# A graph network on 64 graphs: one channel into the stored inputs, loads and a product later, the end of the gates half a graph later

## The chip, the cores and the metric

The kernel runs on one core of a Trainium2 chip. The metric is the device time of one execution in microseconds, as the median of several runs. Beside it there is a profile of one execution. Its engines are TensorE (PE; its weight loads are listed as PEld), VectorE (DVE), ScalarE (ACT), GpSimd (POOL) and SyncE (SP), which only issues DMAs. ACT, POOL and SP each have a queue of DMAs of their own. An engine works through its instructions in the order in which they were put, and a wait stops all that is behind it on this engine.

## The reference

There are 64 graphs of 256 nodes with 256 features each, in float32, and a weighted adjacency matrix for each graph. Layer 0 is a graph convolution with a residual and a norm. Layer 1 has a convolution branch, a distance-weighted message, and a GRU cell. Cut to what matters:

```python
# layer 0
deg = adj.sum(-1);  d = where(deg != 0, deg, 1) ** -0.5
h  = (d[:, :, None] * adj * d[:, None, :] + alpha * eye) @ x
x1 = layernorm(x + h @ W.T + b)
# layer 1, on x1
c  = relu(bn1(conv1(x1)))            # conv1: one tap
c  = relu(bn2(conv2(c)) + x1)        # conv2: 17 taps along the nodes
se = x1 @ w_se.T + b_se              # 3 coordinates per node
A  = exp(-sqdist(se, se)) * adj
m  = A @ relu(x1 @ w_msg.T + b_msg)
h2 = GRU(input=[c, m], state=x1)     # w_ih: 768 x 512, w_hh: 768 x 256
out = layernorm(x1 + h2)
```

## The kernel before

**Stages.** The graphs are worked through one by one (`graphs`), in four quarters of 16 (`Q`). For each graph the first part of the work is layer 0 and then, of layer 1, conv1, the coordinates, the distances and the messages. conv2 is done in the frequency domain, for the 16 graphs of a quarter at once: each graph leaves its transformed columns in `VM`, and when a quarter is complete a long stretch multiplies them with the spectrum of the taps (the products `p_k`, L589, with a block `u` of the spectrum streamed from DRAM by `load_u`, L581, six buffers deep), and transforms back into `xc_d` in DRAM (L782). The spectrum `ud` is made at the start, in the first 280 us, between the first graphs (`taps` loaded by SyncE, products on TensorE, stores by GpSimd). Last come the gates of each graph (`gru`): a product of 256 x 768 by 768 x 1024 (hidden and input weights together), done as seven products of halves instead of eight (`p1`, `p7`, `p6`, `p5` and their like, all at L930; the sums of halves of the inputs on GpSimd at L901, the sums of results on VectorE at L948, L958, L964, L1004).

**Inputs of the gates.** A graph's state and message, transposed, lie in a tile `xn` of 128 x 4 x 256, which ScalarE's queue stores to `xn_d` (L568) at the end of the graph. SyncE loads them later into `inputs` (`load_gate`, L840); it also loads the conv branch (`load_conv`, L830 or L836) and the state untransposed (`load_x1`, L848). While `xn` is in use its first channel of the first row holds ones instead of the state's channel 0, which serve as a row of biases in the products. For 36 of the graphs the residual x1 is added to the conv branch by an accumulating DMA (L860), and TensorE transposes it (L885). For the other 28, which `in_blocks` names (the first four of each quarter and the whole last one), VectorE transposes blocks of 32 x 32 (L872, L874), and GpSimd adds the transposed state out of `inputs` (L875). Channel 0 has ones there and not the state; so it is loaded apart into a tile `channel` (L844) and added by GpSimd (L876), and the bias of the ReLU behind it is one less in this channel (`less_one`).

**The end of the gates.** ScalarE makes the tanh of the candidate (L993); VectorE mixes it with the state (L989 to L995), then takes the norm's statistics (L353, L354); GpSimd takes the power (L356), ScalarE applies the norm (L364), and its queue stores the result (L908). The norm's second part is done in the gates of the graph that follows (`ended`).

**What sets the order.** The pieces are generators. `merge` and `paced` interleave the gates of one quarter with the graphs of the next, so that TensorE has matmuls of the one while the other's chains run: the first quarter's transform goes on beside graphs 16 to 21 (280 to 400 us), the second's and third's beside late gates (555 to 780, 1060 to 1270 us), the early gates beside paced graphs (780 to 1060, 1270 to 1570 us), and gates 36 to 47 beside the end of the last transform (1635 to 1806 us). Gates 48 to 63 come alone, at 14.0 us each, from 1806 us to the end. `tc.issue_after` puts an instruction behind a named one in the order of the same engine. In the first 280 us the weights of the gates are loaded as well (`gate_weights`: 16 pieces of `wall` at L1160, L1161 and L1164, then `hh_top`, `gate_bias` twice and `bn_t`, all on SyncE), taken in stages by the list `others` between the graphs; VectorE folds `hh_top` into `wall` (L1180, L1181) and the biases (L1183, L1184).

Of the kernel before, what the change touches and what calls it, by code (L numbers as in the profile page):

```python
# [14 lines left out]
P = 128  # L15
# [5 lines left out]
def bcast_rows(v, n, rows=P):  # L21

    return bass.AP(tensor=v.tensor, offset=v.offset, ap=[[0, rows], [1, n]])
# [3 lines left out]
def kernel(  # L27
# [79 lines left out]

    def load_x(g):
        xin[g] = loads.tile([P, NCH, D], F32, name="x_t")
        nc.sync.dma_start(xin[g], x[g].rearrange("(c p) f -> p c f", p=P))  # L110

    def load(g):
        if g < B:
# [55 lines left out]
    bn_t = const.tile([P, D], F32)  # L169

    bn2_bias = const.tile([P, DCH], F32)
    less_one = const.tile([P, DCH], F32)

    def batch_norms(pool):

# [197 lines left out]
    xn_d = [dram.tile([P, 2 * DCH, N], F32, name=f"xn_d{g}") for g in range(B)]  # L373
    XN = {}
    ALONE = set()
    EXP, WEIGHED, NORMED = {}, {}, []
    gate = None
    EAGER = {0, Q - 4, Q - 3, Q - 2, *range(Q, Q + 13), 2 * Q + 5, 2 * Q + 6, 3 * Q + 5, 3 * Q + 6}
# [95 lines left out]
    def layer1(g, place):  # L474
# [9 lines left out]
        for c in range(NCH):  # L484
            p = bank("p_conv1")[:, : D + NSE]
            for k in range(DCH):
                nc.tensor.matmul(  # L487
                    p, x1T[:, k, c * P : (c + 1) * P], wc1[:, k, :], start=k == 0, stop=k == DCH - 1
                )
            nc.scalar.activation(  # L490
                h[:, c].rearrange("p (k a) -> p k a", k=DCH), p[:, :D].rearrange("p (a k) -> p k a", k=DCH), AF.Relu
            )
            EVICTED[g] = nc.scalar.copy(cols[:, c, :, :NSE], p[:, D:].unsqueeze(1).to_broadcast([P, 4, NSE])).ins
# [71 lines left out]
                    start=mc == 0, stop=mc == NCH - 1,  # L565
                )
        AGGREGATED[g] = nc.scalar.copy(xn[:, 1 : 1 + DCH], p).ins
        nc.scalar.dma_start(xn_d[g], xn)  # L568
        yield


# [4 lines left out]

    TILES, AWAY = [V], []

    def load_u(n, i):
        u = ustream.tile([P, DCH, D], F32, name="u")  # L580
        nc.sync.dma_start(  # L581
            u, ud[i][n * GC : (n + 1) * GC].rearrange("c g o -> (c g) o")[:D].rearrange("(p k) o -> p k o", k=DCH)
        )
        return u

    def product(p, j, v, u, onto=False):
# [225 lines left out]
            yield from output(q, n + 12, im + 3, re + 3)  # L812


    GATE, CONV, SUMS, OWN, CHANNEL = {}, {}, {}, {}, {}


    EARLY = 4

    def in_blocks(g):  # L820
        return g % Q < EARLY or g >= B - Q

    def load_conv(g):
        y = xc_d[g // Q][g % Q]
        if in_blocks(g):


            CONV[g] = gate.tile([P, DCH, N // RB, RB], F32, name="xc_blocks", tag="xc_g")
            for b in range(NB):
                nc.sync.dma_start(  # L830
                    CONV[g][b * RB : (b + 1) * RB],
                    y.rearrange("(s r) (k b j) -> b r k s j", r=RB, k=DCH, j=RB)[b],
                )
            return
        CONV[g] = gate.tile([P, NCH, D], F32, name="xc_g")
        nc.sync.dma_start(CONV[g], y.rearrange("(c p) d -> p c d", p=P))  # L836

    def load_gate(g):
        inputs = GATE[g] = gate.tile([P, 3 * DCH, N], F32, name="inputs")
        nc.sync.dma_start(inputs[:, : 2 * DCH], xn_d[g])  # L840
        if in_blocks(g):
            CHANNEL[g] = gate.tile([1, N], F32, name="channel", bufs=1)
            with nc.allow_non_contiguous_dma("one channel"):
                nc.sync.dma_start(CHANNEL[g], x1_d[g // Q][g % Q][:, 0:1].rearrange("n d -> d n"))  # L844

    def load_x1(g):
        OWN[g] = gate.tile([P, NCH, D], F32, name="x1_g")
        nc.sync.dma_start(OWN[g], x1_d[g // Q][g % Q].rearrange("(c p) d -> p c d", p=P))  # L848

    def sent(g):  # L850

# [12 lines left out]
    def transposed(g):  # L864

        inputs = GATE[g]
        xcT = inputs[:, 2 * DCH :]
        if in_blocks(g):
            to = xcT.rearrange("p k (s r) -> p k s r", r=RB)
            if g < B - Q:  # L870
                with tc.issue_after(WEIGHED[max(WEIGHED)]):
                    nc.vector.transpose(to, CONV.pop(g))  # L872
            else:
                behind(nc.vector.transpose(to, CONV.pop(g)))  # L874
            nc.gpsimd.tensor_tensor(xcT, xcT, inputs[:, 0 : 2 * DCH : 2 * DCH - 1], op=ALU.add)  # L875
            JOINED.append(nc.gpsimd.tensor_tensor(xcT[0:1, 0], xcT[0:1, 0], CHANNEL.pop(g), op=ALU.add).ins)  # L876
            with tc.issue_after(EXP[max(EXP)]):
                for k in range(DCH):
                    nc.scalar.activation(xcT[:, k], xcT[:, k], AF.Relu, bias=less_one[:, k : k + 1])
            return  # L880
        xc = CONV.pop(g)
        p = bank("p_xcT").rearrange("p (k n) -> p k n", k=DCH)
        for k in range(DCH):
            for c in range(NCH):
                nc.tensor.transpose(p[:, k, c * P : (c + 1) * P], xc[:, c, k * P : (k + 1) * P], ident)  # L885
        for k in range(DCH):
            nc.scalar.activation(xcT[:, k], p[:, k], AF.Relu, bias=bn2_bias[:, k : k + 1])
# [17 lines left out]
    def normed(g, part, y, parts=None):  # L905

        yield from layernorm(y, 4 * LN_EPS, None, parts)
        nc.scalar.dma_start(out[g].rearrange("(c p) d -> p c d", p=P)[:, part], y)  # L908

    def ended():  # L910
        while NORMS:
# [2 lines left out]
    def gru(g):  # L914
# [10 lines left out]
        def product(a, b, p=None):  # L925
            first = p is None
            if first:
                p = accbank("p_g")
            for k in range(HALF):
                nc.tensor.matmul(  # L930
                    p[:, : 3 * HD] if k == 0 else p[:, HD:], a[:, k], wall[:, b, k].rearrange("p t d -> p (t d)"),
                    start=first and k == 0, stop=True, skip_group_check=not first or k > 0,
                )
            return p
# [8 lines left out]
        yield  # L943
        if following:
            sent(g + 1)
        p6 = product(S[2], T2)
        mark(nc.vector.tensor_add(quarter(0, 1), first, p6), 1)  # L947
        nc.vector.tensor_add(quarter(1, 1), quarter(0, 1), p7)  # L948
        product(A12, B21, p1)
# [29 lines left out]
        def mixed(part, cols=slice(0, 2)):  # L979
            both = G[:, part, cols].rearrange("p c h t d -> p (c h) t d")  # L980
            chunks = G[:, part].shape[1]
            r, z, n, i = (both[:, :, j, :] for j in (GR, GZ, GN, GI))
            nc.vector.scalar_tensor_tensor(n, r, 1.0, n, op0=ALU.add, op1=ALU.mult)
            i4 = i.rearrange("p (c h) d -> p c h d", c=chunks)
            bias = bn_t.rearrange("p (h d) -> p h d", h=2)[:, cols]
            nc.vector.tensor_tensor(
                i4, i4, bias.unsqueeze(1).to_broadcast([P, chunks, bias.shape[1], HD]), op=ALU.add
            )
            nc.vector.scalar_tensor_tensor(i, n, 0.5, i, op0=ALU.mult, op1=ALU.add)  # L989
            y = x1[:, part]  # L990
            yq = y.rearrange("p c (h d) -> p c h d", h=2)[:, :, cols].rearrange("p c h d -> p (c h) d")
            mark(nc.vector.scalar_tensor_tensor(yq, z, 3.0, yq, op0=ALU.add, op1=ALU.mult), 1)
            nc.scalar.activation(i, i, AF.Tanh)  # L993
            nc.vector.scalar_tensor_tensor(i, z, 1.0, i, op0=ALU.subtract, op1=ALU.mult)  # L994
            nc.vector.tensor_sub(yq, yq, i)  # L995
            return y

        def finished(part, y):
            NORMS.append(normed(g, part, y))
            next(NORMS[-1])  # L1000

        if g < B - 1:
            squashed(1)
# [118 lines left out]
    with tc.tile_pool(name="setup", bufs=1) as setup:  # L1122
# [31 lines left out]
        nc.gpsimd.tensor_copy(wmsg[0:1, 0], biases[:, NSE:])  # L1154

        def gate_weights():
            for b, i, h in ((B11, 0, 0), (T1, 0, 1), (B21, 1, 0), (B22, 1, 1)):
                at = slice(h * HD, (h + 1) * HD)
                own = w_hhT[i * P : (i + 1) * P].rearrange("p (t d) -> p t d", t=3)
                nc.sync.dma_start(wall[:, b, 0, 0:1], own[:, 2:3, at])  # L1160
                nc.sync.dma_start(wall[:, b, 0, 1:3], own[:, 0:2, at])  # L1161
                for k in range(DCH):
                    row = (D if i == 0 else 0) + k * P
                    nc.sync.dma_start(  # L1164
                        wall[:, b, 1 + k], w_ihT[row : row + P].rearrange("p (t d) -> p t d", t=3)[:, :, at]
                    )
            nc.gpsimd.tensor_copy(less_one, bn2_bias)
            nc.gpsimd.tensor_tensor(less_one[:, 0:1], less_one[:, 0:1], unit, op=ALU.subtract)
            top = setup.tile([P, 3, 2, HD], F32, name="hh_top", tag="taps", bufs=2)
            nc.sync.dma_start(top.rearrange("p t h d -> p (t h d)"), bcast_rows(w_hhT, 3 * D))  # L1170
            rows = setup.tile([1, 2, 3, 2, HD], F32, name="gate_bias", tag="taps", bufs=2)
            for i, v in enumerate((b_hh, b_ih)):
                nc.sync.dma_start(rows[:, i].rearrange("p t h d -> p (t h d)"), v.rearrange("(a d) -> a d", a=1))
            nc.sync.dma_start(bn_t, bcast_rows(b_ih[2 * D :], D))
            yield

            for b, i, h in ((B11, 0, 0), (T1, 0, 1), (B21, 1, 0), (B22, 1, 1)):
# [14 lines left out]
        more_weights = gate_weights()  # L1192
        others = [weights(setup, i, scale2) for i in range(NPARTS)]
        others[0] = later(others[0])
        others += [take(more_weights, i) for i in (1, 3, 2)]
        run(graphs(0, range(Q), others))
    ustream = ctx.enter_context(tc.tile_pool(name="ustream", bufs=6))

# [156 lines left out]
```

## Time and profile before

| | |
|---|---|
| median of 3 runs | 2042.55 us (2040.06 to 2043.63) |
| the profiled execution's own time | 2048.04 us |
| its span in the trace | 2046.3 us |
| TensorE busy, matmuls | 1984.9 us, 8157 |
| VectorE, ScalarE, GpSimd busy | 1396.4, 964.7, 698.1 us |
| DMA: bytes, mean rate | 298.05 MB, 146 GB/s |
| granted TensorE clock | 0.994 |

The profiled execution is one run more, with the recorder on; its span goes from its first to its last instruction, and 1.7 us of its time lie around the span. Busy time of TensorE is modelled at the ends of matmuls, so that matmuls which follow each other closely overlap in the listing, and a stall of TensorE is longer by some tenths than the idle time that is listed.

### The profile page before, as it was taken

How to read it: one execution, taken by the hardware profiler on the slowest of the kernel's cores; microseconds unless marked ns; L12 is line 12 of the kernel's file. 1: busy time of each engine (PE TensorE's matmuls, PEld its weight loads, DVE VectorE, ACT ScalarE, POOL GpSimd, SP SyncE). 2: the span in 40 equal slices, each digit the busy share in tenths (PEclk: the TensorE clock that was granted, in tenths of full speed). 3: DMA queues.
4: the chain of work that ended last, by engine and by line, in shares of the span. 5: the costliest groups of instructions: out<-in, count | busy, mean ns of one | idle time of the engine just before them, and what ended most of it. 6: DMA issues, size and time to landing. Idle time of an engine off the chain costs nothing. (4 is left out here: it accounts for less than half of the span.)

```text
span 2046.3 us, 26391 instructions
## 1 busy us (share of the span) xinstructions
PE 1984.9 (97%) x8157; PEld 1437.7 (70%) x8157; DVE 1396.4 (68%) x3199; ACT 964.7 (47%) x2285; POOL 698.1 (34%) x679
## 2 busy tenths in 40 slices
PE   7999999999999999999999999999999999999997
PEld 6878788878667766777777766777777855555554
DVE  6334447787567788764546888874445899877787
ACT  5666654567442234566653233556664233333333
POOL 4444411232532143223322234322331045445543
PEclk8999999999999999999999999999999999999999
DMA  4766557544555654343336665334344745443431
GB/s 133 221 202 207 182 193 240 169 140 135 138 149 192 212 126 134 115 129 109 103 109 185 211 170 134 119 117 125 97 116 142 259 124 135 127 100 87 102 87 54
DMA packets 269021, 298.05 MB, mean 146 GB/s; under 512 B 84276, under 2 KB 211336, under 8 KB 268882
## 3 DMA queue, kind: packets, MB, share of 16 engines
q1 hardware_dynamic: 208842, 200.37, 33.8%
q10 hardware_dynamic: 44472, 67.39, 9.3%
q0 software_dynamic: 15568, 28.62, 6.3%
q8 instruction: 66, 1.08, 0.2%
q14 instruction: 73, 0.60, 0.1%
HBM read 193.19 MB, written 103.06 MB: 145 GB/s over the span
## 5 line engine op out<-in xcount | busy, mean ns | idle before, releaser
L930 PE MATMUL p_g<-wall,sums 128*128 128x384 f32 x1536 | 534.0, 488 | 6.1 <-POOL sums L901 3.2
L930 PEld LDWEIGHTS p_g<-wall,sums 128*128 128x128 f32 x1536 | 284.8, 190 | 193.4 <-issue 9.6
L930 PE MATMUL p_g<-wall,inputs 128*128 128x384 f32 x1152 | 406.8, 489 | 12.2 <-DVE G L948 12.2
L930 PEld LDWEIGHTS p_g<-wall,inputs 128*128 128x128 f32 x1152 | 215.3, 190 | 167.2 <-DVE G L948 27.8
L356 POOL TENSOR_TENSOR ln_rs<-ln_rs,neg_half 128x2 f32<-128x2 f32 x129 | 95.2, 738 | 546.7 <-DVE ln_rs L355 411.0
L901 POOL TENSOR_TENSOR sums<-inputs 128x384 f32<-128x384 f32 x128 | 143.1, 1118 | 329.0 <-PE p_g L930 303.2
L554 DVE TENSOR_TENSOR aT<-aT,adjT 128x512 f32<-128x512 f32 x64 | 45.2, 706 | 200.5 <-ACT aT L551 200.4
L435 POOL TENSOR_TENSOR x_t<-x_t,b_t 128x512 f32<-128x512 f32 x64 | 101.9, 1592 | 215.3 <-ACT x L432 138.8
L589 PE MATMUL p_k<-u,VM 128*128 128x256 f32 x736 | 169.6, 380 | 2.8 <-DMA u<-ud 1.6
L589 PEld LDWEIGHTS p_k<-u,VM 128*128 128x128 f32 x736 | 138.5, 190 | 25.6 <-PE p_k L589 2.5
L364 ACT ACTIVATE x_g<-x_g,ln_mr,ln_rs 128x256 f32<-128x256 f32 x128 | 70.0, 593 | 169.4 <-DVE ln_mr L360 164.6
L977 ACT ACTIVATE G<-G 128x512 f32<-128x512 f32 (+1 forms) x129 | 81.0, 628 | 128.7 <-DVE G L1004 91.9
L440 PE MATMUL p_hT<-adjT,x 128*128 128x256 f32 x512 | 125.7, 389 | 5.8 <-ACT x L432 2.3
L487 PE MATMUL p_conv<-wc,xn 128*128 128x259 f32 x512 | 126.5, 389 | 4.2 <-ACT xn L471 3.5
L563 PE MATMUL p_nmp<-aT,msg 128*128 128x256 f32 x512 | 121.4, 380 | 2.2 <-DVE aT L554 2.2
L450 PE MATMUL p_out<-w,hT 128*128 128x256 f32 x512 | 121.5, 380 | 0.9 <-ACT hT L445 0.7
L901 POOL TENSOR_TENSOR sums<-inputs,sums 128x384 f32<-128x384 f32 x64 | 74.8, 1169 | 138.0 <-PE p_g L930 137.9
L508 PE MATMUL p_msg<-wmsg,xn 128*128 128x256 f32 x512 | 121.9, 381 | 0.0
L487 PEld LDWEIGHTS p_conv<-wc,xn 128*128 128x128 f32 x512 | 99.1, 194 | 27.1 <-ACT xn L471 4.3
L526 PE MATMUL p_dft<-fwd,h 128*128 128x240 f32 x512 | 114.1, 366 | 0.0
L950 ACT COPY G<-p_g 128x512 f32<-128x512 f32 x64 | 37.4, 584 | 155.9 <-PE p_g L930 107.2
L450 PEld LDWEIGHTS p_out<-w,hT 128*128 128x128 f32 x512 | 95.6, 190 | 21.2 <-ACT hT L445 2.9
(173 smaller groups left out, 3596.9 us busy)
## 6 DMA issues: line engine op xcount, KB each, us to landing
u<-ud SPq DMA_DIRECT2D x284, 256.0 KB
xn_d<-xn ACTq DMA_DIRECT2D x64, 512.0 KB
inputs<-xn_d SPq DMA_DIRECT2D x64, 512.0 KB
ud<-u_set POOLq DMA_DIRECT2D x39, 480.0 KB, 6.3
adj_t<-in_adj_dram SPq DMA_DIRECT2D x64, 256.0 KB
x_t<-in_x_dram SPq DMA_DIRECT2D x64, 256.0 KB
x_d<-x ACTq DMA_DIRECT2D x64, 256.0 KB
xc_d<-VM SPq DMA_DIRECT2D x64, 256.0 KB
```

The costliest lines, as they stand in the source:

```text
L356: nc.gpsimd.tensor_tensor(rs[:, : len(chunks)], rs[:, : len(chunks)], neg_half[:, : len(chunks)], op=ALU.pow)
L435: nc.gpsimd.tensor_tensor(x_t, x_t, b0_t.unsqueeze(1).to_broadcast([P, NCH, D]), op=ALU.add)
L440: nc.tensor.matmul(p[:, k, :], x1[:, mc, k * P : (k + 1) * P], adjT[:, mc, 1 - mc : 3 - mc, :].rearrange("p n q -> p (n q)"), start=mc == ...
L450: nc.tensor.matmul(p[:, c, :], hT[:, k, c * P : (c + 1) * P], w0[:, k, :], start=k == 0, stop=k == DCH - 1)
L487: nc.tensor.matmul(p, x1T[:, k, c * P : (c + 1) * P], wc1[:, k, :], start=k == 0, stop=k == DCH - 1)
L508: nc.tensor.matmul(p[:, c, :], x1T[:, k, c * P : (c + 1) * P], wmsg[:, k, :], start=k == 0, stop=k == DCH - 1)
L526: nc.tensor.matmul(p[:, t0 * FL : t1 * FL], h[:, c, k * P : (k + 1) * P], fwd[:, first : first + t1 - t0, :].rearrange("p t f -> p (t f)") ...
L563: nc.tensor.matmul(p[:, k, :], msg[:, mc, k * P : (k + 1) * P], aT[:, mc].rearrange("p n q -> p (n q)"), start=mc == 0, stop=mc == NCH - 1,)
L589: nc.tensor.matmul(p[:, j * D : (j + 1) * D], v[:, k, :], u[:, k, :], start=k == 0 and j == 0 and not onto, stop=k == DCH - 1, skip_group_ ...
L901: nc.gpsimd.tensor_tensor(S[i], x, y, op=op)
L930: nc.tensor.matmul(p[:, : 3 * HD] if k == 0 else p[:, HD:], a[:, k], wall[:, b, k].rearrange("p t d -> p (t d)"), start=first and k == 0, ...
L977: nc.scalar.activation(rz, rz, AF.Tanh, scale=0.5)
```

## The change

There are five parts.

- **Gate weights.** All loads of `gate_weights` are put behind the last x load that has been issued at this point (`xin["last"]`; in SyncE's order they stand behind graph 16's), and the last third of the spectrum's work and the weights' stages stand in another order in `others`. `less_one` is gone.
- **Channel.** For the 28 graphs of `in_blocks` the store of `xn` is parted: ScalarE's queue stores three of the four parts (1 to 3), SyncE stores rows 1 to 127 of part 0, and a DMA from DRAM to DRAM, on SyncE too, puts the state's channel 0 (a column of `x1_d`) where row 0 is. So `inputs` comes with the state in channel 0; `channel`, its load and its sum are gone. After L875 GpSimd sets row 0 to ones (`memset`), which the products need.
- **Gate loads.** `load_conv`, `load_gate` and `load_x1` are put behind the newest load of `u` (`behind_u`).
- **Sixth product.** In the gates of `in_blocks` graphs below 48, `p6` is put behind the newest matmul of conv1 (`CONV1`).
- **End of the gates.** Below graph 48 the last two steps of the mixing (L994, L995) and the norm's statistics are no longer done at the end of the graph's own gates, but after `p7` in the next graph's (`REST`, `rest`).

The diff:

```diff
     def load_x(g):
         xin[g] = loads.tile([P, NCH, D], F32, name="x_t")
-        nc.sync.dma_start(xin[g], x[g].rearrange("(c p) f -> p c f", p=P))
+        xin["last"] = nc.sync.dma_start(xin[g], x[g].rearrange("(c p) f -> p c f", p=P)).ins
...
-                nc.tensor.matmul(
+                CONV1[g] = nc.tensor.matmul(
                     p, x1T[:, k, c * P : (c + 1) * P], wc1[:, k, :], start=k == 0, stop=k == DCH - 1
-                )
+                ).ins
...
-        nc.scalar.dma_start(xn_d[g], xn)
+        if in_blocks(g):
+            nc.scalar.dma_start(xn_d[g][:, 1:], xn[:, 1:])
+            nc.sync.dma_start(xn_d[g][1:, 0], xn[1:, 0])
+            with nc.allow_non_contiguous_dma("one channel"):
+                nc.sync.dma_start(xn_d[g][0:1, 0], x1_d[g // Q][g % Q][:, 0:1].rearrange("n d -> d n"))
+        else:
+            nc.scalar.dma_start(xn_d[g], xn)
...
+    LAST_U = {}
+    def behind_u():
+        return tc.issue_after(LAST_U[0])
...
     def load_u(n, i):
         u = ustream.tile([P, DCH, D], F32, name="u")
-        nc.sync.dma_start(
+        LAST_U[0] = nc.sync.dma_start(
             u, ud[i][n * GC : (n + 1) * GC].rearrange("c g o -> (c g) o")[:D].rearrange("(p k) o -> p k o", k=DCH)
-        )
+        ).ins
...
     def load_gate(g):
         inputs = GATE[g] = gate.tile([P, 3 * DCH, N], F32, name="inputs")
-        nc.sync.dma_start(inputs[:, : 2 * DCH], xn_d[g])
-        if in_blocks(g):
-            CHANNEL[g] = gate.tile([1, N], F32, name="channel", bufs=1)
-            with nc.allow_non_contiguous_dma("one channel"):
-                nc.sync.dma_start(CHANNEL[g], x1_d[g // Q][g % Q][:, 0:1].rearrange("n d -> d n"))
+        with behind_u():
+            nc.sync.dma_start(inputs[:, : 2 * DCH], xn_d[g])
...
             nc.gpsimd.tensor_tensor(xcT, xcT, inputs[:, 0 : 2 * DCH : 2 * DCH - 1], op=ALU.add)
-            JOINED.append(nc.gpsimd.tensor_tensor(xcT[0:1, 0], xcT[0:1, 0], CHANNEL.pop(g), op=ALU.add).ins)
+            JOINED.append(nc.gpsimd.memset(inputs[0:1, 0], 1.0).ins)
             with tc.issue_after(EXP[max(EXP)]):
                 for k in range(DCH):
-                    nc.scalar.activation(xcT[:, k], xcT[:, k], AF.Relu, bias=less_one[:, k : k + 1])
+                    nc.scalar.activation(xcT[:, k], xcT[:, k], AF.Relu, bias=bn2_bias[:, k : k + 1])
...
+    REST = []
+    def rest():
+        z, i, yq = REST.pop()
+        nc.vector.scalar_tensor_tensor(i, z, 1.0, i, op0=ALU.subtract, op1=ALU.mult)
+        nc.vector.tensor_sub(yq, yq, i)
...
-        p6 = product(S[2], T2)
+        if REST:
+            rest()
+            next(NORMS[-1])
+        with tc.issue_after(CONV1[max(CONV1)]) if in_blocks(g) and g < B - Q else ExitStack():
+            p6 = product(S[2], T2)
...
-            nc.vector.scalar_tensor_tensor(i, z, 1.0, i, op0=ALU.subtract, op1=ALU.mult)
-            nc.vector.tensor_sub(yq, yq, i)
+            REST.append((z, i, yq))
+            if g >= B - Q:
+                rest()
...
-            next(NORMS[-1])
+            if g >= B - Q:
+                next(NORMS[-1])
...
         def gate_weights():
+            behind_x = ExitStack()
+            behind_x.enter_context(tc.issue_after(xin["last"]))
...
-            nc.gpsimd.tensor_copy(less_one, bn2_bias)
-            nc.gpsimd.tensor_tensor(less_one[:, 0:1], less_one[:, 0:1], unit, op=ALU.subtract)
...
+            behind_x.close()
...
         others[0] = later(others[0])
-        others += [take(more_weights, i) for i in (1, 3, 2)]
+        last = others.pop()
+        others += [take(last, 2), chain(later(last), take(more_weights, 1)), take(more_weights, 3), take(more_weights, 2)]
```

`load_conv` and `load_x1` are changed like `load_gate`, and `behind_u` stands around their loads.

## The prediction

> **What bounds it now.** I read the page first, then TensorE's waits, the waits of the engines behind them, and the timeline around each stall that the change touches. Columns of a wait: who waited, for whom, total us, times, longest.
>
> ```profile
> PE 1984.9 (97%) x8157; PEld 1437.7 (70%) x8157; DVE 1396.4 (68%) x3199; ACT 964.7 (47%) x2285; POOL 698.1 (34%) x679
> PE p_g L930 <- DVE G L948: 12.2, 23, 1.5
> PE p_k L589 <- DMA u<-ud: 3.7, 6, 1.3
> PE p_conv L487 <- ACT xn L471: 3.5, 1, 3.5
> PE p_g L930 <- POOL sums L901: 3.2, 2, 1.6
> ```
>
> TensorE is the bound from the first matmul to the last: 1984.9 of 2046.3 us, and the change takes no matmul away. So its worth is only stalls. They are more than the gaps that the page shows, since ends of matmuls are modelled. I therefore took the distance from each matmul's start to the next one's in the timeline, less the median distance for its shape: 87 us of excess in all, 38.4 of it before 520 us, some 5 to 8 in each transform or graph stretch after that, 10.8 from 1635 to 1810, 8.1 behind. Below, "excess" is this. The gates from 1806 us on (240.3 us) aren't touched but for their channel.
>
> **Gate weights behind the last x load.** Before, SyncE issues the loads of `wall` between 65 and 107 us, among the spectra's stores by GpSimd, with the DMA engines 0.91 busy (98 to 108 us). Timeline of ScalarE, then SyncE, then TensorE:
>
> ```profile
> 107.19 0.19 ACT L393 ACTIVATION_READ_ACCUMULATOR adjT<-adj_t 128x1 f32 x1
> 111.93 0.34 ACTq L568 DMA_DIRECT2D xn_d<-xn  x1
> 112.32 0.42 ACT L393 ACTIVATE adjT<-adj_t 128x256 f32<-128x256 f32 x1 [4.93 <-DMA wall<-in_w_hhT_dram]
> ...
> 101.58 3.32 SPq L1161 DMA_DIRECT2D wall<-in_w_hhT_dram  x1
> 104.94 1.84 SPq L1164 DMA_DIRECT2D wall<-in_w_ihT_dram  x2
> ...
> 113.33 2.53 PE L487 MATMUL p_conv<-wc,xn 128*128 128x259 f32 x5 [3.52 <-ACT xn L471]
> ```
>
> ScalarE stood 4.93 us, not for data of its own but because its store `xn_d` (111.93) waited for a `wall` load to end; behind it were L393 and L471, and behind L471 TensorE. Two neighbouring excesses, 3.68 and 0.38: gain 4.1 us.
>
> The 16 `wall` loads, `hh_top`, two rows of biases and `bn_t` now follow graph 16's x load (236.64 us). Behind them in SyncE's queue: graph 17's adj (used at 267.5), its x (used at 272.6), and the first six u (issued at 257.3, used from 279.9). The users are VectorE's four L1180, at 254.0 us before and in the same place of its order now. VectorE is in order, so a late `hh_top` stops what is behind: L401, L360, L497, for which graph 15 waits. From 237 to 257 us the DMA engines are 0.65 (9 us) and 0.47 busy (11 us), so free for 9.0 us. Estimate of the block from packet times in this trace: 16 x 288 packets of 27 ns and 128 of 173 ns (3072 B) over 16 engines are 9.2 us. So it fits just about, and lands at 254 to 257. The dear end: a `wall` load took 1.9 us of SyncE in the busy stretch (99.63 to 101.58); 16 are 30.4 us, landing at 269, 15 us late. Cost 0 to 15 us; I take 2, since the stretch is more like 0.55 busy than 0.91.
>
> **Gate loads behind the newest u (`behind_u`).** SyncE waits at the head of its queue:
>
> ```profile
> SPq L836 <- PE p_xcT L885: 125.8, 22, 25.6
> SPq L844 <- POOL inputs L876: 26.8, 22, 2.6
> ...
> 592.92 0.36 SPq L836 DMA_DIRECT2D xc_g<-xc_d  x1
> 596.83 0.33 SPq L840 DMA_DIRECT2D inputs<-xn_d  x1
> 601.77 0.36 SPq L848 DMA_DIRECT2D x_g<-x_d  x1
> 602.22 5.65 SPq L581 DMA_DIRECT2D u<-ud  x8
> ...
> 605.13 0.70 PE L589 MATMUL p_k<-u,ab 128*128 128x256 f32 x2 [1.25 <-DMA u<-ud]
> ```
>
> Eight u stood ready to be issued behind three gate loads whose buffers were not free; TensorE then waited for the u. The new order puts the u first. Excess there: 1.42 + 0.32, and 1.04 + 0.34 at the same place of the next transform (1093 us): 3.1 us. Four other waits for u (642, 697, 1131, 1186 us, 0.71 to 0.85 each) have no gate load clearly ahead; with them it is 6.2. I take 3.1. Gate loads come a few us later; they are used a gate (14 us) after issue.
>
> **Sixth product later.** In the first early gate of a quarter TensorE stood at p6 for `S[2]`, which GpSimd makes behind L875, L876 and `S[1]`:
>
> ```profile
> 936.93 1.00 POOL L901 TENSOR_TENSOR sums<-inputs 128x384 f32<-128x384 f32 x1 [0.62 <-ACT inputs L879]
> 939.06 1.24 PE L930 MATMUL p_g<-wall,sums 128*128 128x384 f32 x3 [1.62 <-POOL sums L901]
> ```
>
> TensorE's order changes materially at this place and its twin (1428 us) only: conv1 and the distance matmuls go ahead of p6. Excess 1.78 each: gain 3.6. What is late next is L948, the add on p6, and gates' L948 stall TensorE already (12.2 us, 23 times, 0.5 each): 0 to 1.5 per place, taken 0.
>
> **End of the gates and statistics half a graph later (`rest`, L994, L995, L353).** The same instructions, no more. In the early gates VectorE now does a graph's L499, L500, L417 ahead of L994 and L995:
>
> ```profile
> 836.57 0.69 DVE L995 TENSOR_TENSOR x_g<-x_g,G 128x512 f32<-128x512 f32 x1
> 837.25 0.34 DVE L417 SCALAR_TENSOR_TENSOR adjT<-ident,adeg,adjT 128x128 f32<-128x128 f32 x1
> 839.43 0.89 PE L440 MATMUL p_hT<-adjT,x 128*128 128x256 f32 x3 [0.45 <-DVE ln_mv L354]
> ```
>
> Excesses 0.69 (837.5), 0.61 (839.4), 0.98 (914.2), and the three twins at 1327, 1329 and 1403: 4.6 us. From 1635 to 1806 VectorE is busy 159.7 of 171 us, and its order there hardly changes: 0 (to 2). ScalarE's wait that the edit seems aimed at, VectorE L994 for tanh L993 (31.5 us, 26 times), lies for 25.3 us in gates from 48 on, which keep it. Price if the cover goes: the norm's L356 on GpSimd (0.74) and L364 now start after p7 of the next gate, and its store frees `x_g`; SyncE's L848 already waits 213.3 us for these stores. x1 is used some 12 us after issue, so I take 0; without that cover 0.7 per gate over 36 gates, 25 us.
>
> **Channel in the stored inputs.** In 28 graphs: removed, the channel's load (0.54 of SyncE) and L876 (0.73 to 1.05 of GpSimd); added, a memset on GpSimd, nowhere yet on a TensorE path, and two SyncE issues at the graph's end, a store of 127 rows x 1 KB and a column of 256 x 4 B. Nothing here shows a store of 127 rows. Lower bound: spread like the others, 1 KB packets at 46 ns over 16 engines, 0.4 us. Upper bound, all on one engine's ring: 127 x 46 ns = 5.8 us, during which later SyncE loads miss a sixteenth. It counts where u loads follow: graphs 16 to 19 in the first transform, 4 x 0 to 6 us, less the lead of six u (6 to 9 us): 0 to 4 in all. I take 1. Elsewhere x and adj loads are a graph ahead (13 us): 0. SyncE's wait for L876 (26.8 us) goes, but SyncE isn't on the path.
>
> The Trainium skill speaks against this store: by "DMA: Bandwidth & Descriptors", section "Why a DMA increments its semaphore by 16 and not by 1", a transfer started by such a queue uses the largest number of engines up to 16 that divides its slowest dimension, so 127 partitions use one. By it the upper bound would hold at every one of the 28 stores. It is the first thing to look for in the new trace.
>
> **Sum.** -4.1 - 3.1 - 3.6 - 4.6 = -15.4; +2 + 1 = 3; together -12.4. A removed stall of this kind pays fully only if the chain behind it isn't late too. L417's own chain (L401, ScalarE, 0.34) and the next gate's L948 are next within 0.5 us at most places; 8 places x 0.4 = 3.2 come off: -9.2, say -9. The profiled execution (2046.3 span, 1.74 around it, 2048.0) becomes 2039. It is 5.5 above the median of the runs shown, 2042.55; there I forecast 2033.5.
>
> **Rivals.**
> 1. *Late next (no change).* Two thirds of the stalls come back one step later: 15.4 / 3 = 5.1 less the 3 of costs, -2: 2040.5. For: L948 and L958 wait close behind. Against: the 4.1 at 113 us has one cause.
> 2. *The block of weights (slower).* Loads at 1.9 us each: `hh_top` lands at 269 or later, VectorE stands 15 us at L1180, TensorE behind it. In place of the 2 in my -9 that makes +4, and ScalarE's stores (240.6, 254.4), which may wait for such loads as the one at 111.93 did, 2 more: 2048.5. It decides once the block takes over 17 us (237 to 254); the change as a whole is slower once L1180 is over 11 us late, or over 4 together with rival 1. For: the weights stalled an engine once. Against: the DMA engines are half free.
> 3. *All goes well.* Weights free, all six u stalls gone, L948 better too: -15.4 - 3.1 + 0.5: 2024.5.
> 4. *It doesn't do what it says:* gate loads late behind u or out stores, 0.7 per gate over 36 gates, 25 - 9: 2058.
>
> **Chances.** Forecast (2029 to 2038) 0.48, rival 1 0.20, rival 2 0.14, rival 3 0.13, rival 4 0.05. About 0.2% (4.1 us) is what a measurement of this kernel can tell from no change. Faster by over that: forecast and rival 3, and little of rival 1: 0.63. Within: most of rival 1 and some of rival 2: 0.17. Slower: rivals 2 and 4 and a tail: 0.20. The range: from rival 3's 2026 up to rival 2's lower part, 2048.
>
> **What would show it.** Right: no stall of TensorE at 113 us; u issued before `xc_g` near 590; no wait p_g for `sums` L901; L1180 waiting under 4 us near 254. Wrong: VectorE's waits list L1180 for a `wall` or `hh_top` load over 10 us; a new TensorE wait for u between 290 and 390 us behind the 127 rows; p_g's wait for L948 grown past 15; SyncE's L848 much past 213.

## The result, and the profile after

The changed kernel takes 2062.57 us (median of 4 runs, 2059.52 to 2065.26), the kernel before 2043.09 (4 runs). The ratio is 1.0098, 95% interval 1.0078 to 1.0118: some 20 us slower, where 9 us less were forecast. The profiled execution took 2064.5 us, span 2062.7.

Because the two programs run the same 8157 matmuls, their starts can be laid side by side. How much later than before a matmul starts, by the time in the trace of before (worked out from the two timelines, medians over a dozen matmuls):

| at, in before | later by, us | what lies between |
|---|---|---|
| 87 | 5.0 | p_hT late at 69 and 84 |
| 116 | -0.3 | the stall at 113 is gone |
| 246 | -2.5 | |
| 262 | 6.2 | VectorE waits for `hh_top` |
| 331 | 16.9 | three stalls for u |
| 641 | 14.0 | u issued ahead of the gate loads |
| 913 | 13.4 | |
| 949 | 12.0 | sixth product |
| 1269 | 14.4 | a wait for L979, the old L958 |
| 1417 | 10.5 | |
| 1439 | 18.1 | p_conv late |
| 1674 | 22.1 | small steps of 0.8 to 1.3 |
| end | 16.5 | some 6 us come back in the gates from 48 on |

TensorE's waits in the changed kernel, from the page and the view of waits (L947 is the old L930, L605 the old L589, L969 the old L948, L445 the old L440, L492 the old L487, L531 the old L526):

```profile
PE 1992.4 (97%) x8157; PEld 1446.7 (70%) x8157; DVE 1389.0 (67%) x3199; ACT 959.2 (47%) x2285; POOL 688.0 (33%) x677
PE p_g L947 <- DVE G L969: 10.7, 10, 1.7
PE p_hT L445 <- ACT x L437: 8.4, 12, 2.7
PE p_k L605 <- DMA u<-ud: 8.4, 5, 4.1
PE p_conv L492 <- ACT xn L476: 3.9, 1, 3.9
PE p_dft L531 <- ACT scols L498: 3.6, 1, 3.6
```

The wait for u was to fall from 3.7 us and has grown to 8.4; p_hT's has grown from 2.3 to 8.4, and p_dft's is new. The wait for GpSimd's `sums` (3.2) is gone, as forecast.

Waiting is only a part of the loss: TensorE is also busy 7.5 us longer (1992.4 against 1984.9) with the same matmuls. In both traces its granted clock falls to half for 3.4 or 6.8 us beside some of its longer stalls, and the matmuls in such a stretch take nearly twice as long. Eight matmuls of one kind, ahead of the stall at 258 us in the changed kernel and right behind it:

```profile
240.77 1.78 PE L531 MATMUL p_dft<-fwd,h 128*128 128x240 f32 x8
...
258.31 3.33 PE L531 MATMUL p_dft<-fwd,h 128*128 128x240 f32 x8 [3.62 <-ACT scols L498]
```

The mean granted clock in the changed kernel is 0.76 from 85 to 92 us and from 256 to 270, 0.66 from 304 to 314, 0.76 from 1280 to 1287 and 0.66 from 1441 to 1451. In the kernel before it is 0.72 from 112 to 118 and from 245 to 251, and there is no other such stretch but at the start and the end. So the table's steps hold some 8 us of slow matmuls (an estimate: half of TensorE's busy time in these stretches at half clock, 11.6 us against 3.3).

Three places carry most of it. First, the block of weights: SyncE's timeline, the waits of VectorE and ScalarE from 235 to 310 us, and the table of windows (busy time of PE, PEld, DVE, ACT, POOL with counts, clock, DMA share, GB/s).

```profile
236.75 0.47 SPq L1185 DMA_DIRECT2D wall<-in_w_hhT_dram  x1
243.49 4.26 SPq L1189 DMA_DIRECT2D wall<-in_w_ihT_dram  x2
253.90 0.35 SPq L1193 DMA_DIRECT2D hh_top<-in_w_hhT_dram  x1
...
DVE wall L1204 <- DMA hh_top<-in_w_hhT_dram: 7.6, 1, 7.6
ACT unused L398 <- DMA wall<-in_w_ihT_dram: 5.6, 1, 5.6
...
246.00:257.00 11.00, 8.69 (x45) 7.08 (x44) 2.31 (x6) 3.13 (x8) 0.00 (x0) 1.00 0.89 263
```

The block takes SyncE 19 us, from 236.75 to 256, with the DMA engines 0.89 busy where they were 0.47. VectorE could have begun at 251.1 and began at 258.7.

Second, u in the first transform. The view of DMAs from 298 to 312 us, in 40 slices of 0.35 us: tenths of the DMA engines' time that was busy, and GB/s; then TensorE's timeline.

```profile
DMA  9999999721132993000243341223227759999572
GB/s 375 401 407 363 380 340 392 287 88 47 50 46 48 176 158 18 0 0 0 94 41 59 35 35 18 35 41 59 47 41 64 82 170 410 392 357 187 193 298 82
...
307.25 2.08 PE L605 MATMUL p_k<-u,ab 128*128 128x256 f32 x4 [4.11 <-DMA u<-ud]
```

While TensorE stands for u (303.1 to 307.25 us), the DMAs move at most 94 GB/s from 303.25 on, where the first slices show 340 to 407. The 1 KB packets of the row store (issued at 291.79) come at 24 in each microsecond, about one every 42 ns: one engine's pace, where a spread load shows over a hundred. The column of 256 x 4 B was issued at 300.70, ahead of the trough.

Third, near 1440 us. Two row stores (1417 and 1421) are followed by an x load that SyncE needed 8.1 us to issue; as the profile infers it, ScalarE's next `xn_d` store waited for this load, as the one at 111.93 us had done for a wall load, and TensorE for ScalarE:

```profile
1421.45 0.24 SPq L575 DMA_DIRECT2D xn_d<-xn  x1
1422.71 8.10 SPq L110 DMA_DIRECT2D x_t<-in_x_dram  x1
...
1442.53 0.42 ACT L398 ACTIVATE unused<-adj_t 128x256 f32<-128x256 f32 x1 [5.62 <-DMA x_t<-in_x_dram]
...
1443.54 2.96 PE L492 MATMUL p_conv<-wc,xn 128*128 128x259 f32 x6 [3.90 <-ACT xn L476]
```

### The profile page after: what moved, and what is told of

The parts are those of the page before. It is cut to its first block, busy times and chain, and to the rows that moved or that the text cites. A ratio compares the mean times of both kernels' runs of the same rounds, so it can differ in the third digit from the quotient of the medians.

```text
span 2062.7 us, 26441 instructions
## 1 busy us (share of the span) xinstructions
PE 1992.4 (97%) x8157; PEld 1446.7 (70%) x8157; DVE 1389.0 (67%) x3199; ACT 959.2 (47%) x2285; POOL 688.0 (33%) x677
## 4 chain that ended last, share of the span: by engine, by line
PE 76%; DVE 12%; DMA 6%; ACT 2%; issue 2%; SPq 1%; POOL 1%; ACTq 0%; POOLq 0%; DVEq 0%
PE p_g L947 34%; PE p_k L605 11%; PE p_hT L445 5%; PE p_out L455 4%; PE p_conv L492 4%; PE p_nmp L568 4%; PE p_msg L513 4%; PE p_dft L531 3%; PE p_u L329 2%; DMA u<-ud 2%; PE p_dist L555 2%; PE p_x1T L475 1%; DMA x_t<-in_x_dram 1%; PE p_adjT L419 1%; DVE VM L797 1%
## 5 line engine op out<-in xcount | busy, mean ns | idle before, releaser
L947 PE MATMUL p_g<-wall,sums 128*128 128x384 f32 x1536 | 535.5, 490 | 5.1 <-DVE G L979 4.0
L947 PEld LDWEIGHTS p_g<-wall,sums 128*128 128x128 f32 x1536 | 286.3, 191 | 192.4 <-issue 14.3
L947 PE MATMUL p_g<-wall,inputs 128*128 128x384 f32 x1152 | 406.2, 489 | 11.0 <-DVE G L969 10.7
L947 PEld LDWEIGHTS p_g<-wall,inputs 128*128 128x128 f32 x1152 | 216.4, 190 | 165.1 <-DVE G L969 24.8
L911 POOL TENSOR_TENSOR sums<-inputs 128x384 f32<-128x384 f32 x128 | 151.3, 1183 | 225.7 <-PE p_g L947 204.5
L605 PE MATMUL p_k<-u,VM 128*128 128x256 f32 x736 | 171.7, 384 | 4.7 <-DMA u<-ud 3.4
L440 POOL TENSOR_TENSOR x_t<-x_t,b_t 128x512 f32<-128x512 f32 x64 | 99.1, 1549 | 230.5 <-ACT x L437 149.3
L605 PEld LDWEIGHTS p_k<-u,VM 128*128 128x128 f32 x736 | 140.2, 192 | 28.1 <-ACT ab L651 3.6
L445 PE MATMUL p_hT<-adjT,x 128*128 128x256 f32 x512 | 128.2, 396 | 9.3 <-ACT x L437 8.4
L492 PE MATMUL p_conv<-wc,xn 128*128 128x259 f32 x512 | 126.4, 390 | 4.6 <-ACT xn L476 3.9
L531 PE MATMUL p_dft<-fwd,h 128*128 128x240 f32 x512 | 116.1, 370 | 3.7 <-ACT scols L498 3.6
L492 PEld LDWEIGHTS p_conv<-wc,xn 128*128 128x128 f32 x512 | 99.2, 194 | 27.3 <-ACT xn L476 4.9
L445 PEld LDWEIGHTS p_hT<-adjT,x 128*128 128x128 f32 x512 | 95.3, 197 | 26.7 <-ACT x L437 14.6
```

The source lines that it names most:

```text
L440: nc.gpsimd.tensor_tensor(x_t, x_t, b0_t.unsqueeze(1).to_broadcast([P, NCH, D]), op=ALU.add)
L445: nc.tensor.matmul(p[:, k, :], x1[:, mc, k * P : (k + 1) * P], adjT[:, mc, 1 - mc : 3 - mc, :].rearrange("p n q -> p (n q)"), start=mc == ...
L492: CONV1[g] = nc.tensor.matmul(p, x1T[:, k, c * P : (c + 1) * P], wc1[:, k, :], start=k == 0, stop=k == DCH - 1).ins
L531: nc.tensor.matmul(p[:, t0 * FL : t1 * FL], h[:, c, k * P : (k + 1) * P], fwd[:, first : first + t1 - t0, :].rearrange("p t f -> p (t f)") ...
L605: nc.tensor.matmul(p[:, j * D : (j + 1) * D], v[:, k, :], u[:, k, :], start=k == 0 and j == 0 and not onto, stop=k == DCH - 1, skip_group_ ...
L911: nc.gpsimd.tensor_tensor(S[i], x, y, op=op)
```

## The experiments

Two theories at first: the block of weights costs 8 us, and the store of 127 rows, on one DMA engine, the rest. The trace of the first runs brought a third suspect, the column of 4-byte pieces. Every time is a median of its runs, with the ratio to the runs of the kernel before on the same chip and its 95% interval. A loss or gain at a place is worked out from the starts of matmuls, as in the table above, in the time of the trace of before.

### Weights as before (e1)

```diff
-            behind_x.enter_context(tc.issue_after(xin["last"]))
...
-        last = others.pop()
-        others += [take(last, 2), chain(later(last), take(more_weights, 1)), take(more_weights, 3), take(more_weights, 2)]
+        others += [take(more_weights, i) for i in (1, 3, 2)]
```

> The changed kernel with the loads of the gate weights and the order of the stages as they were before; all else as changed. Theory 1 (two causes: the block of weights, and the store of 127 rows on one DMA engine): the VectorE wait of 7.6 us for hh_top and the four TensorE stalls behind it (some 8.5 us) go, a wait of ScalarE for a wall load near 110 us comes back (up to 4): 2055 to 2058 us, no wait of VectorE for hh_top; the stalls for u at 307 and 346 us and the 3.9 us stall of p_conv near 1440 stay. Rival (the row store alone slows, the weights only fill time that it opened): less than 2 us from the changed kernel's 2062.6.

2064.97 us, ratio 1.0104 (1.0078 to 1.0130). By the total the rival won; by the trace neither did. VectorE's wait for `hh_top` is gone, and from 245 to 266 us 8.9 us come back beside the changed kernel. But by 245 us this kernel was 7.7 us later. The wall loads now stood among the early row stores and columns, with two new waits of p_conv for ScalarE (3.6 together), and 2.6 us that the changed kernel had gained near 246 were not gained here. With the channel's part in place, moving the weights back bought nothing in all.

### Rows in 112 and 15 (e2), and both (e3)

```diff
-            nc.sync.dma_start(xn_d[g][1:, 0], xn[1:, 0])
+            nc.sync.dma_start(xn_d[g][1:113, 0], xn[1:113, 0])
+            nc.sync.dma_start(xn_d[g][113:, 0], xn[113:, 0])
```

> The changed kernel with the store of rows 1 to 127 in two DMAs, rows 1 to 112 and 113 to 127. Theory 1: 1 KB packets of these stores come at the rate of 15 or 16 engines and not of one; the u stalls at 307, 346 and 348 us (7.2 us), those of p_hT at 69 and 87 us (4.3) and of p_conv at 1440 (4.1) go: -12 to -16, so 2047 to 2051 us; VectorE's wait of 7.6 us for hh_top stays. Rival (the weights alone, the stalls for u follow from the shift in time): within 3 us of 2062.6, the u stalls stay. Second rival (SyncE is held by its new waits for xn and x_d, not by the packets): the u stalls stay too, though the packets are spread.

> Both edits of the two runs beside it: weights as before, row store in 112 and 15 rows. Theory 1: the sum of the two, -17 to -22: 2040 to 2046 us; and if the three parts that are left bring the 11 us that were forecast for them, near 2034. Rival (the parts left cost as much as they bring): 2043 or more.

e2: 2053.14 us, ratio 1.0050 (1.0030 to 1.0070), 9.4 less than the changed kernel. The stalls at 87 us (4.5) and 1440 (4.1 and 2.2) went, as expected; the stalls for u stayed, 7.5 us in the first transform, which was not. e3: 2048.47 us, 1.0033 (1.0013 to 1.0053), the rival's number: still slower than before, with 7.5 us of stalls for u. So a second cause lay at u, and a view of e3's DMAs showed the trough again, behind the column.

### Weights alone (e4) and channel alone (e5)

e4 is the kernel before with the part of the weights alone, e5 with that of the channel alone, both as in the change's diff.

> The kernel before with the weights' part alone: their loads behind graph 16's x load, and the new order of the stages. Theory 1: VectorE waits 5 to 8 us for hh_top near 255 us and TensorE some 8 behind it, the 4.1 us at 113 go: +4, near 2047 us. Rival (the block hurts only together with the row store): the 4.1 us are gained, 2039.

> The kernel before with the channel's part alone, as changed (127 rows in one store, column from DRAM to DRAM). Theory 1: TensorE stalls near 70 to 110 us (4 to 8), for u in the first transform (7 to 11) and near 1430 (4); in the gates from 48 on some 5 us less, since the changed kernel lost 5 there and only this part touches them: net +10 to +18, 2053 to 2061. Rival (the forecast's +1): within 3 us of 2043. If the 5 us from 48 on do not come, something else than the channel brought them.

e4: 2052.26 us, 1.0042 (1.0026 to 1.0059). By the medians that is 9.9 more than before, where +4 was expected. VectorE waits 7.0 us for `hh_top`, and 8.2 us are lost between 250 and 262 us. e5: 2067.07 us, 1.0124 (1.0097 to 1.0151), 23.5 more than before, above the range of either theory: 9.8 us near 84 us, 7.2 near 296, 3.3 near 330. Nothing is lost near 1440 us here, nor with the rows alone (e15 below), so that stall needs the other parts beside the store. The channel's part is the worst by far; the us that come back from 48 on (5.9 here) are in e5 too, so the channel brings them.

### No column (e7)

```diff
-            nc.sync.dma_start(xn_d[g][1:113, 0], xn[1:113, 0])
-            nc.sync.dma_start(xn_d[g][113:, 0], xn[113:, 0])
-            with nc.allow_non_contiguous_dma("one channel"):
-                nc.sync.dma_start(xn_d[g][0:1, 0], x1_d[g // Q][g % Q][:, 0:1].rearrange("n d -> d n"))
+            nc.sync.dma_start(xn_d[g][:, 0], xn[:, 0])
```

> Weights as before; SyncE stores all 128 rows of the state's part of xn in one DMA, and the column from DRAM to DRAM is left out. It leaves part of the computation out: channel 0 of the 28 graphs is one in the residual. Beside the run with 112 and 15 rows (2048.5). Theory 2 (the column of 256 x 4 B stops the queue: after it, DMA engines stood nearly idle for 7 us with u waiting): the u stalls at 297 (4.3) and 333 us (3.2) go: 2039 to 2042 us. Rival (SyncE held by its wait for xn, which is still there): the u stalls stay at 4 and 3 us, 2047 to 2049.

This kernel leaves channel 0 of the 28 graphs out of the residual, and has the rows in one store of 128 in place of 112 and 15. 2027.1 us, 0.9925 (0.9910 to 0.9940): 21 us less than e3, and 16 faster than the kernel before. No stall for u is left in the first transform. SyncE still waits for `xn` there (its waits from 270 to 345 us), so that wait was not the cause:

```profile
SPq L575 <- ACT xn L477: 8.2, 3, 3.8
```

### The column and the rows, each by itself (e14, e15)

To the kernel before, at the same places, into a scratch tensor that nothing reads:

```diff
         nc.scalar.dma_start(xn_d[g], xn)
+        if g % Q < 4 or g >= B - Q:
+            nc.sync.dma_start(extra_d[g][0:1], x1_d[g // Q][g % Q][:, 0:1].rearrange("n d -> d n"))   # e14
+            nc.sync.dma_start(extra_d[g][1:], xn[1:, 0])                                             # e15
```

> The kernel before, all as it was, and besides 28 columns of 256 x 4 B from DRAM to DRAM at the places of the change, into a scratch tensor that nothing reads: the disputed cost by itself. Theory 2: +10 to +17 (u stalls near 300 and 335 us, DMA engines idle behind the column), 2053 to 2060. Rival (it hurts only with the row stores): under +3, 2046.

> The kernel before, all as it was, and besides 28 stores of 127 rows x 1 KB on SyncE at the places of the change, into a scratch tensor that nothing reads. Theory 1 (one DMA engine takes all of it, 5 to 6 us, and what is behind it waits): +8 to +13 (stalls near 70 to 90, 300 and 1430 us), 2051 to 2056. Rival (the ring has room, only the column costs): under +3, 2046.

e14: 2065.73 us, 1.0114 (1.0099 to 1.0130). 28 kilobytes in all cost 24 us, more than theory 2 expected: 9.6 of them near 85 us, 10 between 290 and 365 us at the loads of u, some 2.5 near 1095. e15: 2052.7 us, 1.0052 (1.0037 to 1.0067): 28 stores of 127 KB cost 11, most of it (8.7 us) from 78 to 97 us, where a store of 127 rows stands ahead of the adj, wall and taps loads; at u TensorE waits 0.2.

### What in the column (e16, e17, e18)

Again added to the kernel before: e16 the same column, but into a tile of 16 x 16; e17 one row of 1 KB from DRAM to DRAM; e18 the column of e14 on ScalarE's queue.

```diff
+            nc.sync.dma_start(ch, x1_d[g // Q][g % Q][:, 0:1].rearrange("(a n) d -> a (n d)", a=16))    # e16
+            nc.sync.dma_start(extra_d[g][0:1], x1_d[g // Q][g % Q][0:1])                               # e17
+            nc.scalar.dma_start(extra_d[g][0:1], x1_d[g // Q][g % Q][:, 0:1].rearrange("n d -> d n"))   # e18
```

> The kernel before and besides the 28 columns of 256 x 4 B, at the places of the change, but loaded into a small tile that nothing reads (16 x 16) in place of DRAM. Theory 2a (the 4-byte writes to DRAM stop the queue): within 4 us of 2043. Theory 2b (the reads of 4 bytes at a stride of 1 KB, or SyncE's wait for the store of x1, do it): +15 to +24 like the column from DRAM to DRAM (2065.7).

> The kernel before and besides 28 copies of one row of 1 KB from DRAM to DRAM at the places of the change (same wait for the store of x1, one piece in place of 256). Theory 2 (256 small pieces): within 4 us of 2043. Rival (SyncE's wait for x1's store, or a copy from DRAM to DRAM as such): +15 to +24.

> The kernel before and besides the 28 columns from DRAM to DRAM on ScalarE's queue in place of SyncE's. Theory 2 as a queue's matter (what stands behind the column in the same queue waits): the u stalls near 300 and 335 us go, under +6, 2049; ScalarE itself may wait for x1's store. Rival (the pieces hold the DMA engines whatever the queue): u stalls as before it, +15 to +24.

e16: 2044.61 us, 1.0010 (0.9998 to 1.0023); e17: 2044.98, 1.0014 (1.0005 to 1.0024): next to nothing. e18: 2066.87, 1.0121 (1.0102 to 1.0141). So on SyncE's queue it is neither the 4-byte reads (e16) nor SyncE's wait for x1's store (e17), but the 256 pieces of 4 bytes written to DRAM. The tile of e16 has 16 rows and the target of e14 one, but this is not the difference: in the kernel before, the channel's load puts as many pieces into one row of SBUF, and behind the one issued at 1425.41 us the DMAs moved 345 to 435 GB/s from 1427.75 on.

The total of e18 is as dear as e14's, but not by the same path. 12.6 us of it are lost before 74 us, where ScalarE itself waits for x1's store ahead of the column. At u, with the columns on the other queue, TensorE still waits 4.2 us, against 7.4 in e14 (both from 280 to 400 us). First ScalarE in e18, then TensorE in e18 and in e14:

```profile
ACT hT L446 <- DMA x_d<-x: 15.8, 3, 6.4
PE p_k L593 <- DMA u<-ud: 4.2, 2, 2.4
PE p_k L593 <- DMA u<-ud: 7.4, 4, 4.2
```

So the pieces hold up loads of another queue too; how much of their price is the place in a queue is not told apart.

The DMAs just behind a column, in e14 (295 to 311 us) and then in e16 (289 to 305), slices of 0.4 us:

```profile
DMA  1002471004645312330212879999999977157800
GB/s 72 26 0 2 42 143 61 0 0 15 26 87 67 26 20 26 36 36 20 31 31 41 87 261 405 405 410 399 399 405 369 215 189 287 51 46 246 333 31 0
```

```profile
DMA  4997007888799796899820000029789879897587
GB/s 169 399 379 277 0 5 67 312 297 113 292 384 374 246 276 149 287 343 358 323 108 0 0 0 0 0 26 164 282 307 307 215 230 282 297 307 251 210 343 277
```

With the writes to DRAM (issued at 295.11) the loads of u crawl for some 6 us at 15 to 87 GB/s (from 298.6 to 304.2) and then run at 400; the pieces themselves are listed with 9 ns each, and give nothing away. In e16 the same 256 pieces (issued at 286.85) leave no such trough. The Trainium skill, "DMA: Bandwidth & Descriptors", section "Specifications", states that transfers below 512 B are done as read-modify-write. By this line alone e16 would be hit like e14, and its ratio is 1.0010, so it does not tell the two apart. What the memory does with the pieces no run here shows.

### Three parts alone (e8), and mended versions (e10, e12, e13)

e8 is the kernel before with gate loads behind u, the sixth product later and the end of the gates later, as in the change's diff. e10 has these three, the channel for graphs 48 to 63 alone with rows of 112 and 15, and the weights spread:

```diff
-            for b, i, h in ((B11, 0, 0), (T1, 0, 1), (B21, 1, 0), (B22, 1, 1)):
+            for n, (b, i, h) in enumerate(((B11, 0, 0), (T1, 0, 1), (B21, 1, 0), (B22, 1, 1))):
+                behind_x = ExitStack()
+                behind_x.enter_context(tc.issue_after(XLOADS[(9, 11, 13, 15)[n]]))
```

> The kernel before with three parts alone: gate loads behind u, sixth product later, end of the gates half a graph later; channel and weights as before. Theory of the prediction: -11.3, 2032 us. Rival (late next: in the changed kernel two stalls on L979 behind longer VectorE operations grew from 1 to 2.1 us, and those before gate 48 grew by 1.6): -4 to -7, 2036 to 2039.

> A mended change: wall loads in four parts behind the x loads of graphs 9, 11, 13 and 15; the channel in the stored inputs for graphs 48 to 63 alone, rows in 112 and 15; the three other parts as changed. Theory 1 with the rivals of the runs beside it: -4 to -7 of the three parts, -4 at 113 and up to -4 more from an early stretch without weight loads, -5 in the gates from 48 on: -13 to -19, 2024 to 2030. If VectorE waits for hh_top again or the column stalls the queue in the graph stretch too: 2035 or more.

e8: 2035.67 us, 0.9968 (0.9957 to 0.9979), 7.9 less than before: just past the rival's band of 4 to 7, and short of the 11.3 of the prediction. e10: 2027.36 us, 0.9925 (0.9909 to 0.9942), inside its band. VectorE doesn't wait for `hh_top` in e10. In e12 the channel of all 28 graphs comes as one row out of PSUM, the rows are in 112 and 15, and the weights are spread:

```diff
+            nc.scalar.copy(ch, p[0:1, 0])
+            nc.sync.dma_start(xn_d[g][0:1, 0], ch)
...
-                nc.sync.dma_start(xn_d[g][0:1, 0], x1_d[g // Q][g % Q][:, 0:1].rearrange("n d -> d n"))
```

> The changed kernel with the wall loads spread over four x loads, rows in 112 and 15, and for all 28 graphs the state's channel 0 copied by ScalarE out of PSUM into a tile of one row, which SyncE stores as one row of 1 KB in place of the column from DRAM to DRAM. Theory 2 (the 256 writes of 4 bytes from DRAM to DRAM stop the queue): no u stall over 1 us in the first transform, 2024 to 2029 us, like the run without a column (2027.1). Rival (SyncE's waits at a graph's end hold the u): u stalls of 4 and 3 us as in the run with 112 and 15 rows, 2035 to 2042.

2028.55 us, 0.9933 (0.9918 to 0.9948), without a stall for u in the first transform: the whole change runs 13 us faster than the kernel before, once the column is a row, the rows are spread and the weights too. In e13 the end of the gates is later only below graph 36, all else as in e10:

```diff
-            if g >= B - Q:
+            if g >= B - Q - 12:
                 rest()
```

> The mended kernel (2027.4) with the end of the gates half a graph later only below graph 36, so that gates 36 to 47 are as before. Theory 3 (in the dense stretch L994, L995 and the statistics now stand right ahead of the add L948 on which TensorE waits: five steps of 1.0 to 1.1 us there): -4 to -5, 2022 to 2024; TensorE's wait for L948 from 1590 us to gate 48 falls from about 9.7 to 7.6. Rival (the steps come from the gate loads behind u or from the shift in time): no change, within 1.5 us.

2025.53 us, 0.9918 (0.9901 to 0.9934). That is 1.8 us below e10, where 4 to 5 were expected. But e10 ran on another chip, where the kernel before was 2.1 us slower, and the two ratios differ by 0.0007, less than their intervals: by its time e13 is not told apart from e10. TensorE's waits from about 1570 to 1800 us, in the kernel before, then in e10 and in e13 (1585 to 1813 in the first; the line numbers name the same add, `quarter(1, 1)` with `p7`):

```profile
PE p_g L930 <- DVE G L948: 7.6, 7, 1.5
```

```profile
PE p_g L959 <- DVE G L981: 9.0, 8, 1.6
PE p_g L959 <- DVE G L981: 7.9, 8, 1.5
```

The wait falls by 1.1 from e10 to e13, nearly to its old size, as the theory says. But e8 loses 5.3 us on the kernel before from 1580 to 1876 (e16, which leaves the end of the gates as it was, loses 1.4), and the rest of this is not explained by this wait.

## Why the prediction was wrong

**Channel: the step that failed.** The forecast was +1 us (0 to 4); alone it cost 23.5 (e5). Two terms were mis-sized, and one was missing. The 127 rows on one engine were in the text, with the right duration, but were counted only where u loads follow; e15 shows 0.2 there and 8.7 in the first 100 us, where SyncE's early loads and spectrum's stores had no slack. "Elsewhere x and adj loads are a graph ahead: 0" was wrong also at 1440, where, with all parts in place, stores at 1417 and 1421 followed each other and took ScalarE's store along. The column had no term: "a column of 256 x 4 B" was named and priced at nothing, without a reason; by itself it cost 24 (e14). The only row of before that is near, the channel's load with as many pieces, wrote to SBUF: it could price the reading of a column, not the writing of one to DRAM.

**What follows a stall.** The prediction counted stalls alone, and no term held the matmuls at half clock behind a new one, some 8 us in the changed kernel. It could have been read in the trace of before: at 113 us the two excesses that it took, 3.68 and 0.38, are followed by six matmuls that are late by 0.21 each, 5.4 in all.

**The rule on 127 rows.** The Trainium skill's rule that the prediction cites held: the packets came at one engine's pace, 24 in a microsecond. But of the cost it was the smaller part, 9 by e2 and 11 by e15, against 24 for the column by e14. The costs of parts do not add up: the weights alone (9.9), the channel alone (23.5) and the other three (-7.9) make 25.5, and the whole change cost 19.5; this difference was not traced.

**Weights.** Rival 2's mechanism came, at its place: 19 us where the bound was 17, VectorE 7.6 us late, ScalarE late too (5.6). I took 2; it was 8.2 at this place (e4). The term that failed is the cover: "free for 9.0 us" took the block's packets at 27 ns as if they could fill every gap, and the block needed all of the 20 us at 0.87 to 0.89 busy.

**The gain of 4.1 us at 113 us.** It was not there to be had. In e8, where the loads stand as before, ScalarE waits at this place for the same load only:

```profile
ACT adjT L399 <- DMA wall<-in_w_hhT_dram: 1.3, 1, 1.3
```

The stall of 4.93 us belonged to the one execution that was profiled, which was 5.5 us above its median. Every later trace, of whatever kernel, gains 4.1 to 5.4 us on it between 100 and 130 us, also those whose loads stand as before (e8, e14 to e18). A stall that hangs on the landing of one DMA should have been discounted by this difference.

**u, sixth product, end of the gates.** These were forecast at 3.1 + 3.6 + 4.6 = 11.3. e8 against before shows 3.8 for the sixth product (1.9 at each place) and 4.7 for the end of the gates, both at the places named. For u it shows 2.0 at 603 us. The other place, 1093, was a miss: TensorE's wait for u there (0.88 before) is still 0.84 in e8, and what e8 gains from there to 1133 (1.3) is gained by e16 as well, with the loads in their old order. Given back are 5.3 us from 1580 to 1876 (1.4 of them in e16 too), where I had taken 0. The 1.6 that e8 loses near 1267, at a wait for L958, can't be booked to "late next": this wait is 2.0 us in e14 and e18, which leave the end of the gates as it was, and 0.9 in e7 and e12, which change it. What was left is -7.9 by the medians. The discount of 3.2 was of the right kind and too small.

**GpSimd's L876: a gain taken at 0.** In the gates from 48 on TensorE waited 4.3 us for L948 before, and 0.4 in e10, whose channel differs there:

```profile
1884.54 1.05 POOL L876 TENSOR_TENSOR inputs<-inputs,channel 1x256 f32<-1x256 f32 x1
...
1886.68 0.69 DVE L994 SCALAR_TENSOR_TENSOR G<-G 128x512 f32<-128x512 f32 x1 [1.68 <-ACT G L993]
```

```profile
1905.32 0.30 POOL L886 MEMSET inputs<- 1x256 f32 x1
...
1907.23 0.69 DVE L924 SCALAR_TENSOR_TENSOR G<-G 128x512 f32<-128x512 f32 x1 [1.42 <-ACT G L1014]
```

The first pair is the kernel before, the second the changed one. The ReLU no longer waits for L876, and VectorE's wait for the tanh is 0.26 us shorter in the gate shown. The usual wait of these gates is 1.67 in the kernel before and in e8, whose channel is as before, and 1.42 in the changed kernel and in e10. Times 16 gates that would be 4.2, the size of what TensorE got back; this is an estimate, since some gates wait less in every run. That ScalarE's ReLU, ahead of the tanh in its order, is the link was read off the order, not tried.

**The range.** It names "rival 3's 2026" as its lower end, where rival 3's own sum is 2024.5; nothing hangs on it here.

## What to carry to other kernels

Price a DMA by the side that it writes as well as the side that it reads, and by each queue and engine it holds: a small piece that is cheap into SBUF can be dear into DRAM, and its own packets don't show it, only the throughput behind them does. Before a stall is booked as a gain, compare the profiled execution with the median: what it is above may be just this stall. A block of loads that fitted the mean of the free bandwidth did not fit its gaps; spread over four places it cost no wait (e10). And when a stall is priced, look at the matmuls behind it too.

## What the runs showed of the hardware

28 writes of 256 pieces of 4 B to DRAM (28 KB) through SyncE's queue cost 24 us (e14). Through ScalarE's queue the cost was 24.5, but 12.6 us of it were lost where ScalarE waited for another store (e18). With the same pieces written to SBUF the time was 1.0010 of before (e16), and with one piece of 1 KB 1.0014 (e17). Behind such a column the loads of u fell to 15 to 87 GB/s for some 6 us. A store of 127 partitions moved 24 packets of 1 KB in a microsecond; split in 112 and 15 rows the stalls behind it, other than those for u, went. Beside TensorE stalls of 2.0 to 4.1 us in the changed kernel its granted clock was half for 3.4 or 6.8 us, and eight matmuls took 3.33 us in place of 1.78; the same wait of 1.98 us was followed by such a stretch at 1282 us and not at 795.
